# Mask halves half a batch earlier from the middle of the loop on, and another order of bias, ReLU and residual in the last tile

## The chip, the cores and the metric

The kernel runs on one core of a Trainium2 chip. Such a core has a matrix engine (TensorE, in the profile PE), three engines for elementwise work (VectorE or DVE, ScalarE or ACT, GpSimd or POOL), a queue that only issues transfers (SyncE or SP), and 16 DMA engines. All of them work through their own list of instructions in order, and wait for each other by semaphores. The metric is the device time of one execution in microseconds (us): the median of the runs.

## The reference

A layer of graph attention on x [16 batches, 512 nodes, 512 features], a conditioning vector per batch and an integer mask [16, 512, 512, 11]. Only the first 20 nodes of each batch are attended to.

```python
row_zero = exp_v.sum(-1) == 0
q_exp = jnp.where(row_zero[..., None], 0.0, q[:, None, :])
self_feat = concatenate([exp_v, q_exp], -1) @ W_self.T + b_self
output = self_feat
for d in range(2):
    A = adj_f if d == 0 else jnp.swapaxes(adj_f, 1, 2)
    A = A[:, :, :NONGT, :]                 # NONGT = 20
    cond = A.sum(-1)
    vb = A @ w_bias + b_bias
    output = output + _gat_attention(self_feat, cond, vb, ...)
return exp_v + jax.nn.relu(output)

# _gat_attention, 16 heads of 32, kv = self_feat[:, :20]
aff = jnp.einsum('bnhd,bmhd->bnhm', qh, kh) * (1.0 / np.sqrt(dh))
aff = jnp.where(cond_adj[:, :, None, :] > 0, aff, NEG) + label_bias[:, :, None, :]
w = jax.nn.softmax(aff, axis=-1)
out = jnp.einsum('bnhm,bmf->bnhf', w, kv) @ Wout + bout
```

So each batch needs the self features, the scores of 512 nodes against 2 x 16 x 20 keys, an additive mask from the integers, a softmax over each group of 20, the weighted sum of value rows, and at the end bias, ReLU and the addition of x.

## The kernel before

Features lie on the 128 partitions: a batch of x is a tile of 128 x 4 x 512 (four feature chunks, 512 nodes). A setup stage of about 107 us folds the weights into per-batch keys (`g`, kept in device memory as `g_d`) and per-batch value rows (`vw_d`). Then the main loop goes over 16 batches `b` and, in each, over four stages `nt` of 128 nodes. A mask half `(b, h)` covers two stages: half 0 the stages 0 and 1, half 1 the stages 2 and 3.

The order of the work is written out by hand: the calls of the loop body are recorded in program order, and each engine gets its own instructions in that order. What a stage issues is, in this order:

- SP: `store()` of finished output (L338), then loads. In stage 0 the rows of x for the row sums of batch b+2 (`load_xn`, L89). In stage 1 the mask half (b+1, 0) (`load_adj`, L93), then the per-key bias (`load_cq`, L100), and in batch 0 also `clear_blocks` (L126, six DMAs) and `blocks` (L142, twelve DMAs), which lay out all batches' value rows in `bd_d`. In stage 2 the values (`load_values`, L114), the keys of b+1 (L108), x of b+2 (L85) and the mask half (b+1, 1).
- `normal` of the stage before: VectorE sums the exponentials and takes reciprocals (L291, L292), POOL multiplies (L293).
- TensorE: `self_feat` (L186), the products for self features; in stages 0 and 1 for the second half of the nodes of this batch, in stage 3 for the first half of the nodes of the next. In stage 2 also `attend` (L311) of the batch before, into four banks, followed by `finish` (L324 on VectorE, L330 on ScalarE). Then `scores` (L246).
- mask work. `mask_mul`: ScalarE casts the integers (L207), POOL multiplies them by `w_bias` (L208). `mask_count`: VectorE counts (L213) and turns the count into 0 or a very negative number (L214). `mask_add`, a stage later: VectorE sums the products (L220) and adds the count's part (L222), ScalarE spreads the result over `both` (L227).
- `self_copy`: VectorE moves self features out of PSUM, adding the conditioning term (L199). The scores of later stages read them.
- `weigh` and `expo`: VectorE adds the mask, takes the maximum and subtracts it (L257, L259, L261), ScalarE exponentiates (L266).
- `turn` of the stage before: VectorE transposes the weights (L300); `full_add` for the next stage on POOL (L236), which joins `cq` and `both`; in stages 2 and 3 `residual` on POOL (L333), which adds x.

Buffers that matter: `ps_s` (scores) has two, `ps_acc` four. The four of `ps_acc` are shared by the results of `self_feat` and the four banks of `attend`. Mask integers (`adj`) have three, their products (`prod`) one, `both` two.

The last tile is the output of batch 15, after the loop. `attend` is split in two parts: nodes 0 to 383 from the first three stages and nodes 384 to 511 from the last. VectorE adds self features to each bank (L685), ScalarE adds the bias `bo` and applies ReLU (L689), then x is added: on POOL for chunks 0 to 2 of the first part (L692), on VectorE for the second part (L695) and for chunk 3 of the first (L698). All stores are issued by SP.

Of the kernel before, what the change touches and what calls it, by code (L numbers as in the profile page):

```python
# [9 lines left out]
AF = mybir.ActivationFunctionType  # L10
ALU = mybir.AluOpType
# [7 lines left out]
def gat_kernel(  # L19
# [20 lines left out]
    nc = tc.nc  # L40
    B, F, N = xT.shape
    NG, L = adj.shape[3], adj.shape[4]
    H, DH = 16, 32
    C = F // P
    HL = P // DH
    NT = N // P
# [10 lines left out]
    load = ctx.enter_context(tc.tile_pool(name="load", bufs=2))  # L57
# [7 lines left out]
    bo = const.tile([P, C], F32, name="bo")  # L65
# [13 lines left out]
    xs, xns, rss, adjs, nzs, sfs, cqs, gs, vds = {}, {}, {}, {}, {}, {}, {}, {}, {}  # L79
# [11 lines left out]
    def load_adj(b, h):  # L91
        t = adjs[b, h] = load.tile([P, 2, S * L], I32, tag="adj", name=f"adj{b}_{h}", bufs=3)
        nc.sync.dma_start(  # L93
            t, adj[b, h * 2 * P : (h + 1) * 2 * P].rearrange("(t p) d m l -> p t (d m l)", p=P)
        )
# [108 lines left out]
    def mask_mul(b, h):  # L204
        a = adjs[b, h]
        p = prods[b, h] = msk.tile([P, 2 * S, L], F32, tag="prod", name=f"prod{b}_{h}", bufs=1)
        nc.scalar.copy(p.rearrange("p m l -> p (m l)"), a.rearrange("p t m -> p (t m)"))  # L207
        nc.gpsimd.tensor_mul(p, p, wb_sb.unsqueeze(1).to_broadcast([P, 2 * S, L]))  # L208

    def mask_count(b, h):  # L210
        a = adjs.pop((b, h))
        cond = conds[b, h] = msk.tile([P, 2 * S], F32, tag="cond", name=f"cond{b}_{h}")
        nc.vector.tensor_reduce(cond, a.rearrange("p t (m l) -> p (t m) l", l=L), AX.X, ALU.add)  # L213
        nc.vector.tensor_scalar(cond, cond, 0.0, NEG, ALU.is_le, ALU.mult)  # L214

    def mask_add(b, h):

        nm = 2 * S
        lb = msk.tile([P, nm], F32, tag="lb", name=f"lb{b}_{h}")
        nc.vector.tensor_reduce(lb, prods.pop((b, h)), AX.X, ALU.add)  # L220
        add = msk.tile([P, nm], F32, tag="add", name=f"add{b}_{h}")
        nc.vector.scalar_tensor_tensor(add, conds.pop((b, h)), bb_sb, lb, ALU.add, ALU.add)  # L222

        both = adds[b, h] = msk.tile([P, 2, 2, S], F32, tag="both", name=f"both{b}_{h}")
        for a in range(2):
            for g in range(2):
                nc.scalar.copy(  # L227
                    both[bass.ts(a, R), :, g], add[bass.ts(g, R)].rearrange("p (t m) -> p t m", t=2)
                )
# [344 lines left out]
    with tc.manual_schedule():  # L574
        load_keys(1)

        prev = None
        o = None
        banks = None
        for b in range(B):  # L580
            def ahead(nt):


                if nt < 2:
                    return ((b, nt, 1),)
                return ((b + 1, 0, 0), (b + 1, 1, 0)) if nt == 3 and b + 1 < B else ()

            for nt in range(NT):
                store()
                if nt == 0 and b + 2 < B:  # L590
                    load_xn(b + 2, 0)
                    load_xn(b + 2, 1)
                if nt == 1:
                    if b + 1 < B:
                        load_adj(b + 1, 0)
                        load_cq(b + 1)
                    if b == 0:
                        clear_blocks(zero)
                        blocks()
                if nt == 2:  # L600
                    load_values(b)
                    if 0 < b < B - 1:
                        load_keys(b + 1)
                    if b + 2 < B:
                        load_x(b + 2)
                    if b + 1 < B:
                        load_adj(b + 1, 1)

                if prev is not None:
                    normal(*prev)  # L610
                ps = ps_s.tile([P, 2, 512], F32, tag="s", name=f"ps_s{b}_{nt}")
                for part in ahead(nt):
                    self_feat(*part)
                if nt == 2 and b > 0:
                    banks = [ps_acc.tile([P, 512], F32, tag="acc", name=f"ps_o{b - 1}_{q}") for q in range(4)]
                    for n in range(2):
                        attend(b - 1, n, [t[:, bass.ts(n, N // 2)] for t in banks])
                    o = work.tile([P, C, N], F32, tag="o", name=f"o{b - 1}")
                    finish(b - 1, o, (0, 1), banks)
                for g in range(2):  # L620
                    scores(b, nt, g, ps)

                if nt == 0:
                    mask_mul(b, 1)
                    mask_count(b, 1)
                if nt == 1:
                    mask_add(b, 1)
                if nt == 2 and b + 1 < B:
                    mask_mul(b + 1, 0)
                    mask_count(b + 1, 0)  # L630
                if nt == 3 and b + 1 < B:
                    mask_add(b + 1, 0)
                last = b == B - 1
                for part in ahead(nt):
                    self_copy(*part)
                if nt == 3 and b + 2 < B:
                    row_mask(b + 2)
                if last and nt == NT - 1:
                    s = soft.tile(full, F32, tag="s", name=f"s{b}_{nt}", bufs=3)
                    weigh_half(b, nt, ps, s, 0)  # L640
                    turn(*prev)
                    weigh_half(b, nt, ps, s, 1)
                else:
                    s = weigh(b, nt, ps)
                    expo(s)
                    if prev is not None:
                        turn(*prev)
                if nt < NT - 1:
                    full_add(b, nt + 1)
                elif b + 1 < B:  # L650
                    full_add(b + 1, 0)
                if nt >= 2 and b > 0:
                    residual(b - 1, 2 * nt - 4, o)
                    residual(b - 1, 2 * nt - 3, o)
                if b + 2 < B:
                    if 0 < nt < 3:
                        row_sum(b + 2, 2 * nt - 2)
                        row_sum(b + 2, 2 * nt - 1)
                    if nt == 3:
                        load_nz(b + 2)  # L660
                prev = (b, nt, s)
        store()
        b = B - 1
        turn_half(*prev, 0)
        turn_half(*prev, 1)

        o = work.tile([P, C, N], F32, tag="o", name=f"o{b}")
        out_b = out[b].rearrange("(c p) n -> p c n", p=P)
        most = [ps_acc.tile([P, 512], F32, tag="acc", name=f"ps_o{b}_{q}") for q in range(4)]
        pairs = [ps_s.tile([P, 2, 512], F32, tag="s", name=f"ps_o{b}_{q}_2") for q in range(2)]  # L670
        rest = [pairs[q // 2][:, q % 2] for q in range(4)]
        parts = []
        for lo, hi, banks in ((0, NT - 1, most), (NT - 1, NT, rest)):
            width = (hi - lo) * R
            parts.append((slice(2 * lo, 2 * hi), slice(lo * P, hi * P), width, banks))
            for n in range(2):
                attend(b, n, [t[:, bass.ts(n, width)] for t in banks], slice(lo, hi))
        for ts, ns, width, banks in parts:
            for q in range(4):
                c = bass.ds(q // 2 * 2, 2)  # L680

                def of(t):
                    return t[:, c].rearrange("p c (t q n) -> p c t q n", q=2, n=32)[:, :, ts, q % 2]

                nc.vector.tensor_add(  # L685
                    of(o), banks[q][:, : 2 * width].rearrange("p (c t n) -> p c t n", c=2, n=32), of(sfs[b])
                )
            for c in range(C):
                nc.scalar.activation(o[:, c, ns], o[:, c, ns], AF.Relu, bias=bo[:, c : c + 1])  # L689
        ns = parts[0][1]  # L690
        for c in range(3):
            nc.gpsimd.tensor_add(o[:, c, ns], o[:, c, ns], xs[b][:, c, ns])  # L692
            nc.sync.dma_start(out_b[:, c, ns], o[:, c, ns])
        ns = parts[1][1]
        nc.vector.tensor_add(o[:, :, ns], o[:, :, ns], xs[b][:, :, ns])  # L695
        nc.sync.dma_start(out_b[:, :, ns], o[:, :, ns])
        ns = parts[0][1]
        nc.vector.tensor_add(o[:, 3, ns], o[:, 3, ns], xs[b][:, 3, ns])  # L698
        nc.sync.dma_start(out_b[:, 3, ns], o[:, 3, ns])


# [44 lines left out]
```

## Time and profile before

| | |
|---|---|
| median of 3 runs | 647.06 us |
| lowest and highest run | 645.69 and 651.63 us |
| the profiled execution | 648.63 us |
| its span, first to last instruction | 646.5 us |
| busy: PE, DVE, POOL, ACT | 627.9, 522.8, 337.0, 217.4 us |
| mean granted clock of TensorE | 0.986 |
| one batch in the loop | 33.3 us |

Busy time is the time in which an engine executes an instruction; the weight loads of TensorE have their own row, PEld, and run beside its products. The page cuts the span into 40 slices of about 16 us and gives a digit for each: the busy share in tenths, or the granted clock in tenths of full speed. Lines of the timeline have the start, the length, the engine, the line of the kernel, the operation, what it writes and reads, and in brackets the idle time just before it and what ended it. Instructions of one kind in close succession are merged in such a line. The chain that ended last is followed back from the last instruction, at each step to what released it.

### The profile page before, as it was taken

How to read it: one execution, taken by the hardware profiler on the slowest of the kernel's cores; microseconds unless marked ns; L12 is line 12 of the kernel's file. 1: busy time of each engine (PE TensorE's matmuls, PEld its weight loads, DVE VectorE, ACT ScalarE, POOL GpSimd, SP SyncE). 2: the span in 40 equal slices, each digit the busy share in tenths (PEclk: the TensorE clock that was granted, in tenths of full speed). 3: DMA queues.
4: the chain of work that ended last, by engine and by line, in shares of the span. 5: the costliest groups of instructions: out<-in, count | busy, mean ns of one | idle time of the engine just before them, and what ended most of it. 6: DMA issues, size and time to landing. Idle time of an engine off the chain costs nothing.

```text
span 646.5 us, 16155 instructions
## 1 busy us (share of the span) xinstructions
PE 627.9 (97%) x6742; PEld 378.7 (59%) x6742; DVE 522.8 (81%) x802; ACT 217.4 (34%) x468; POOL 337.0 (52%) x254
## 2 busy tenths in 40 slices
PE   9998989999999999999999999999999999999992
PEld 7653336876656565656565656565656565656552
DVE  0644472899899898989898989898989898989896
ACT  0342341324233342425242425252525151523232
POOL 1420222442838374757474756556565647474754
PEclk9898998999999999999999999999999999999997
DMA  8939998766646464647464757475656566634112
GB/s 316 398 127 327 390 379 286 226 174 219 218 153 212 160 221 151 233 142 230 151 224 154 238 154 240 154 240 153 230 164 220 175 208 186 207 122 144 66 67 99
DMA packets 89888, 131.86 MB, mean 204 GB/s; under 512 B 9208, under 2 KB 59928, under 8 KB 87768
## 3 DMA queue, kind: packets, MB, share of 16 engines
q1 hardware_dynamic: 89144, 129.47, 60.0%
q0 software_dynamic: 672, 1.36, 0.8%
q8 instruction: 53, 0.87, 0.5%
q14 instruction: 19, 0.16, 0.1%
HBM read 90.89 MB, written 39.92 MB: 202 GB/s over the span
## 4 chain that ended last, share of the span: by engine, by line
PE 82%; DVE 2%; DMA 1%; ACT 1%; issue 0%; SPq 0%; DVEq 0%; ACTq 0%
PE ps_s L246 42%; PE ps_sf L186 32%; PE ps_o L311 6%; PE ps_g L518 1%; DMA g_d<-st 1%; ACT o L689 0%; DVE st L527 0%; SPq L532 0%; PE ps_v L492 0%; DVE s L284 0%; DVE mx L275 0%; DVE o L685 0%; DVE s L276 0%; DVE ps_s L273 0%; DVE wt L300 0%
## 5 line engine op out<-in xcount | busy, mean ns | idle before, releaser
L246 PE MATMUL ps_s<-g,sf 128*64 128x320 f32 x2048 | 289.1, 433 | 0.0
L186 PE MATMUL ps_sf<-x,ws_v 128*64 128x256 f32 (+1 forms) x2048 | 225.2, 372 | 0.0
L246 PEld LDWEIGHTS ps_s<-g,sf 128*64 128x64 f32 x2048 | 154.8, 137 | 118.0 <-issue 6.2
L186 PEld LDWEIGHTS ps_sf<-x,ws_v 128*64 128x64 f32 x2048 | 149.1, 137 | 71.9 <-issue 4.2
L293 POOL TENSOR_TENSOR s<-s,sm 128x640 f32<-128x640 f32 x63 | 80.2, 1273 | 151.0 <-DVE sm L292 133.5
L266 ACT ACTIVATE s<-s 128x640 f32<-128x640 f32 x63 | 46.5, 738 | 239.7 <-DVE s L261 239.7
L236 POOL TENSOR_TENSOR full<-cq,both 128x640 f32<-128x640 f32 x64 | 99.1, 1550 | 23.5 <-ACT both L227 23.5
L208 POOL TENSOR_TENSOR prod<-prod,wb_sb 128x880 f32<-128x880 f32 x32 | 61.4, 1918 | 60.9 <-ACT prod L207 60.9
L257 DVE TENSOR_TENSOR ps_s<-ps_s,full 128x640 f32<-128x640 f32 x63 | 52.3, 830 | 42.6 <-PE ps_s L246 42.5
L333 POOL TENSOR_TENSOR o<-o,x 128x512 f32<-128x512 f32 x60 | 75.3, 1277 | 0.0
L227 ACT COPY both<-add 64x80 f32<-64x80 f32 x128 | 32.8, 256 | 75.9 <-DVE add L222 74.8
L527 DVE TENSOR_SCALAR st<-ps_g 128x640 f32<-128x640 f32 x32 | 26.4, 824 | 37.8 <-PE ps_g L518 31.7
L291 DVE TENSOR_REDUCE sm<-s 128x32 f32<-128x640 f32 x63 | 51.7, 820 | 6.0 <-ACT s L266 0.9
L199 DVE SCALAR_TENSOR_TENSOR sf<-nz,qw,ps_sf 128x236 f32<-128x236 f32 (+1 forms) x128 | 52.6, 458 | 2.8 <-PE ps_sf L186 2.6
L259 DVE TENSOR_REDUCE mx<-ps_s 128x32 f32<-128x640 f32 x63 | 51.9, 825 | 2.2
L261 DVE TENSOR_TENSOR s<-ps_s,mx 128x640 f32<-128x640 f32 x63 | 51.9, 824 | 2.2
L300 DVE STREAM_TRANSPOSE wt<-s 128x640 f32<-128x640 f32 x63 | 52.5, 834 | 0.0
L311 PE MATMUL ps_o<-wt,vd 32*32 32x256 f32 (+2 forms) x2176 | 46.3, 374 | 5.6 <-issue 3.3
L330 ACT ACTIVATE o<-o,bo 128x512 f32<-128x512 f32 x60 | 40.0, 714 | 27.4 <-DVE o L324 24.9
L311 PEld LDWEIGHTS ps_o<-wt,vd 32*32 32x32 f32 x2176 | 31.0, 103 | 21.3 <-issue 13.8
L324 DVE TENSOR_TENSOR o<-ps_o,sf 128x512 f32<-128x512 f32 x60 | 36.3, 666 | 0.0
L525 ACT ACTIVATE st<-ps_g 128x640 f32<-128x640 f32 x32 | 22.4, 704 | 37.4 <-PE ps_g L518 29.5
(70 smaller groups left out, 422.1 us busy)
## 6 DMA issues: line engine op xcount, KB each, us to landing
g<-g_d SPq DMA_DIRECT2D x15, 1280.0 KB, 7.1
g_d<-st SPq DMA_DIRECT2D x16, 1120.0 KB, 6.1
x<-in_xT SPq DMA_DIRECT2D x16, 1024.0 KB, 9.2
out_T<-o SPq DMA_DIRECT2D x61, 256.0 KB, 2.0
xn<-in_xn SPq DMA_DIRECT2D x28, 512.0 KB, 6.7
adj<-in_adj SPq DMA_DIRECT2D x32, 440.0 KB, 8.1
vd<-bd_d SPq DMA_DIRECT2D x64, 128.0 KB, 2.6
nz<-nz_d SPq DMA_DIRECT2D x14, 256.0 KB, 4.5
```

Source lines behind the costliest of these rows:

```text
L186: nc.tensor.matmul(held[0][bass.ts(a, R), i * N // 2 : i * N // 2 + hi - lo], ws_v[:, k, bass.ds((2 * f + i) * P + a * R, R)], xs[b][:, k, ...
L199: nc.vector.scalar_tensor_tensor(sfs[b][:, 2 * f + i, lo:hi], nzs[b][:, lo:hi], qw[:, 2 * f + i, b : b + 1], ps[:, i * N // 2 : i * N // 2 ...
L208: nc.gpsimd.tensor_mul(p, p, wb_sb.unsqueeze(1).to_broadcast([P, 2 * S, L]))
L236: nc.gpsimd.tensor_add(f, cqs[b].unsqueeze(1).to_broadcast(shape), adds[b, nt // 2][:, nt % 2].unsqueeze(2).to_broadcast(shape),)
L246: nc.tensor.matmul(ps[bass.ts(a, R), g, : W // 2], sfs[b][:, k, bass.ds(nt * P + g * R, R)], keys[:, k, a], start=(k == 0), stop=(k == C - 1),
L257: nc.vector.tensor_add(pw, pw, fulls.pop((b, nt)).rearrange("p g h m -> p g (h m)"))
L259: nc.vector.tensor_reduce(mx, p4, AX.X, ALU.max)
L261: nc.vector.tensor_sub(s, p4, mx.unsqueeze(3).to_broadcast(full))
L293: nc.gpsimd.tensor_mul(s, s, sm.unsqueeze(3).to_broadcast(full))
L300: nc.vector.transpose(wts[b][:, nt], s.rearrange("p a h m -> p (a h m)"))
L311: nc.tensor.matmul(banks[q][bass.ts(e, DH)].rearrange("p (t n) -> p t n", n=32), vds[b][r, e, i, q // 2 * 2 + n], wt[r, :, bass.ts(j, 32)] ...
L333: nc.gpsimd.tensor_add(o[:, c], o[:, c], xs[b][:, c])
```

## The change

A table, `mask_plan`, is made ahead of the loop. It says for each stage which mask half is loaded, which is multiplied and counted, and which is added. Up to batch 7 it gives each half the stages it had. Batch B // 2 = 8 takes a third half, so that from there on every half comes half a batch earlier; in batch 15 there is none left. In a stage of batch 8 that has both, the addition comes ahead of the next half's multiplication and count. The loads of the table are made after the other loads of the stage: in stage 1 after `load_cq`, and in batch 0 after `clear_blocks` and `blocks`.

In the last tile ScalarE writes self features plus bias into `o` ahead of time, for all four chunks. VectorE then adds the banks to `o`. Chunks 0 to 2 of the first part have ReLU on ScalarE and x added on POOL as before; the second part and chunk 3 of the first have ReLU and the addition of x in one VectorE operation (`scalar_tensor_tensor`, maximum with 0, then add). The store of the second part is issued by ScalarE.

```diff
+        mask_plan = {(b, nt): [] for b in range(B) for nt in range(NT)}
+        m = 1
+        for b in range(B):
+            for nt in (0, 1, 2) if b == B // 2 else (0, 2):
+                if m < 2 * B:
+                    half = (m // 2, m % 2)
+                    if m > 1:
+                        mask_plan[(b, nt - 1) if nt else (b - 1, 2)].append(("load", half))
+                    mask_plan[b, nt].append(("mul", half))
+                    mask_plan[b, nt + 1].insert(0, ("add", half))
+                    m += 1
...
                 if nt == 1:
                     if b + 1 < B:
-                        load_adj(b + 1, 0)
                         load_cq(b + 1)
                     if b == 0:
                         clear_blocks(zero)
                         blocks()
...
-                    if b + 1 < B:
-                        load_adj(b + 1, 1)
+                for what, m in mask_plan[b, nt]:
+                    if what == "load":
+                        load_adj(*m)
...
-                if nt == 0:
-                    mask_mul(b, 1)
-                    mask_count(b, 1)
-                if nt == 1:
-                    mask_add(b, 1)
-                if nt == 2 and b + 1 < B:
-                    mask_mul(b + 1, 0)
-                    mask_count(b + 1, 0)
-                if nt == 3 and b + 1 < B:
-                    mask_add(b + 1, 0)
+                for what, m in mask_plan[b, nt]:
+                    if what == "add":
+                        mask_add(*m)
+                    elif what == "mul":
+                        mask_mul(*m)
+                        mask_count(*m)
...
         o = work.tile([P, C, N], F32, tag="o", name=f"o{b}")
+        for c in range(C):
+            nc.scalar.activation(o[:, c], sfs[b][:, c], AF.Identity, bias=bo[:, c : c + 1])
...
                 nc.vector.tensor_add(
-                    of(o), banks[q][:, : 2 * width].rearrange("p (c t n) -> p c t n", c=2, n=32), of(sfs[b])
+                    of(o), banks[q][:, : 2 * width].rearrange("p (c t n) -> p c t n", c=2, n=32), of(o)
                 )
-            for c in range(C):
-                nc.scalar.activation(o[:, c, ns], o[:, c, ns], AF.Relu, bias=bo[:, c : c + 1])
+
+        def end(queue, cs, ns):
+            nc.vector.scalar_tensor_tensor(
+                o[:, cs, ns], o[:, cs, ns], 0.0, xs[b][:, cs, ns], ALU.max, ALU.add
+            )
+            queue.dma_start(out_b[:, cs, ns], o[:, cs, ns])
+
         ns = parts[0][1]
         for c in range(3):
+            nc.scalar.activation(o[:, c, ns], o[:, c, ns], AF.Relu)
             nc.gpsimd.tensor_add(o[:, c, ns], o[:, c, ns], xs[b][:, c, ns])
             nc.sync.dma_start(out_b[:, c, ns], o[:, c, ns])
-        ns = parts[1][1]
-        nc.vector.tensor_add(o[:, :, ns], o[:, :, ns], xs[b][:, :, ns])
-        nc.sync.dma_start(out_b[:, :, ns], o[:, :, ns])
-        ns = parts[0][1]
-        nc.vector.tensor_add(o[:, 3, ns], o[:, 3, ns], xs[b][:, 3, ns])
-        nc.sync.dma_start(out_b[:, 3, ns], o[:, 3, ns])
+        end(nc.scalar, slice(0, C), parts[1][1])
+        end(nc.sync, slice(3, C), ns)
```

## The prediction

> **What bounds the kernel now.** I read the page's engine row first, then the clock row, then the chain that ended last.
>
> ```profile
> PE 627.9 (97%) x6742; PEld 378.7 (59%) x6742; DVE 522.8 (81%) x802; ACT 217.4 (34%) x468; POOL 337.0 (52%) x254
> PEclk9898998999999999999999999999999999999997
> PE 82%; DVE 2%; DMA 1%; ACT 1%; issue 0%; SPq 0%; DVEq 0%; ACTq 0%
> ```
>
> The chain is TensorE (PE) for 82% of the span, at full granted clock from the eighth slice to the last but one. So in the batch loop an instruction saved on another engine is worth nothing, and an instruction added costs only where TensorE then waits. Two places decide: stretches where VectorE (DVE) is nearly late, and the tail after the last scores (about 630 us), where the chain leaves TensorE. VectorE's spare time in the loop is 42.5 us of waiting for scores over 45 waits, just under 1 us a time.
>
> One batch takes 33.3 us, so batch 0 starts at about 107 us and batch 8 at about 373 us. Next I read the SP queue at the start of the loop, since the diff moves a load there (start, length, engine, line, operation, count).
>
> ```profile
> 111.45 0.44 SPq L93 DMA_DIRECT2D adj<-in_adj  x1
> ...
> 113.98 6.65 SPq L126 DMA_DIRECT2D bd_d<-zero  x6
> 120.80 9.42 SPq L142 DMA_DIRECT2D bd_d<-vw_d  x12
> 132.48 1.72 SPq L114 DMA_DIRECT2D vd<-bd_d  x4
> ...
> 134.72 0.50 SPq L93 DMA_DIRECT2D adj<-in_adj  x1
> ```
>
> The load of mask half (1,0) is issued at 111.45, ahead of the 18 DMAs of `clear_blocks` and `blocks`; these hold the queue until 130.22. Then VectorE over the same batches:
>
> ```profile
> 124.75 1.01 DVE L213 TENSOR_REDUCE cond<-adj 128x80 f32<-128x880 int32 x1
> ...
> 132.21 1.56 DVE L199 SCALAR_TENSOR_TENSOR sf<-nz,qw,ps_sf 128x236 f32<-128x236 f32 x4
> ...
> 140.98 1.07 DVE L213 TENSOR_REDUCE cond<-adj 128x80 f32<-128x880 int32 x1 [1.10 <-DMA adj<-in_adj]
> 142.08 1.92 DVE L214 TENSOR_SCALAR cond<-cond 128x80 f32<-128x80 f32 x1
> ...
> 150.70 0.86 DVE L199 SCALAR_TENSOR_TENSOR sf<-nz,qw,ps_sf 128x256 f32<-128x256 f32 x2
> ```
>
> At 124.75 VectorE reads half (1,0). Apart from the 1.10 us for half (1,1), it works without a pause until 151.56, when the self copy of (1,1,1) ends. TensorE:
>
> ```profile
> 138.00 0.43 PE L246 MATMUL ps_s<-g,sf 128*64 128x320 f32 x1
> ...
> 150.59 0.63 PE L311 MATMUL ps_o<-wt,vd 32*32 32x256 f32 x6
> 151.66 2.69 PE L311 MATMUL ps_o<-wt,vd 32*32 32x256 f32 x122 [0.44 <-issue]
> ```
>
> Scores of batch 1 start at 138.00; `attend(0)` starts at 150.59, stops after a few matmuls and goes on at 151.66, 0.1 us after that self copy. The reason is in the code: `attend` takes all four buffers of `ps_acc`, and the fourth still holds ps_sf(1,1,1). So here VectorE already sets TensorE's time, with no slack at all.
>
> **Part 1, the load of half (1,0).** In the new loop the loads of the plan stand behind the `nt == 1` block. For every batch that puts the mask load behind two cq loads, 2 us later, which costs nothing: in batch 7 it is issued at 341.80 and read at 358.71. In batch 0 it also puts it behind `clear_blocks` and `blocks`: 18 DMAs, 6.65 + 9.42 us of issue. When does it land? The queue loses the load's own 0.49 us and the 0.7 us for which a clear waited for that load to land, so it ends between 129.0 and 130.2; I take 129.2. From issue to landing no row shows this load alone. Below: 2.6 us (vd, 128 KB). Above: 6.3 us (issue 134.72, read 140.98, behind vd and 1 MB of x). Taking out that megabyte at the page's best rate of 398 GB/s, 2.6 us, and adding 0.4 us for the last bd_d packets gives 4.1 us. So it lands at 133.3, between 131.6 and 136.5.
>
> VectorE comes to its count at 124.75 and now waits until 133.3. Queued behind it are `weigh(0,2)`, `normal(0,2)`, the mask sum, the four self copies of batch 1 and all that follows; ScalarE waits at the cast of the same half, and POOL behind that cast. From the count to the self copy's end at 151.56 the old trace has 26.81 us, 1.10 of it the DMA wait, which goes since half (1,1) then lands first. The 1.92 us of the second L214 instead of 0.51 lies beside POOL's product of 1.91 us that the same landing released; it moves to half (1,0), so it stays in the sum. New end: 133.3 + 25.7 = 159.0. TensorE's own way there: it stops after self_feat at 138.0, since the first self copy now comes at 132.21 + 8.6 + 1.4 + 0.4 = 142.6; from there 4.3 + 3.5 + 4.3 us of work bring it to 154.7, where it waits again until 159.0. Against 151.56: **+7.5 us** (+5.7 to +10.6 by the landing). Behind that point TensorE runs without a pause in the old trace and VectorE falls in step with it, so nothing is won back.
>
> Here a rule counts. The page "TensorE: Matmul & The Clock Gate" of the Trainium skill (sections "Why this matters for your kernels" and "Part 1") says that after an idle gap of over about 3 us the array drops to half clock, and comes back after a window of about 3.4 us. The trace has gaps of up to 1 us in the loop and a full clock there, so it shows neither. By the row alone the two new gaps (4.6 and 4.3 us) cost what was summed. By the rule the first costs up to 1.7 us more, hidden in the second gap; a drop after the second gap would add 1.7 us. Since a drop in the first shortens the second to 2.6 us, I leave it out and keep it for the range.
>
> **Part 2, batch 8 takes three halves.** Per half VectorE has 1.01 + 0.5 (count) and 1.01 + 0.55 (sum), ScalarE 0.91 + 1.06, POOL 1.92.
>
> ```profile
> 383.43 0.86 DVE L199 SCALAR_TENSOR_TENSOR sf<-nz,qw,ps_sf 128x256 f32<-128x256 f32 x2
> ...
> 385.00 2.75 PE L311 MATMUL ps_o<-wt,vd 32*32 32x256 f32 x128
> ```
>
> In stage 1 the count of half (9,0) now stands ahead of this self copy, the one that `attend` waits for: it ends at 384.29 + 1.3 = 385.6 instead, 0.5 us after `attend` wants its fourth buffer. Half (9,0) is issued at 374.17 as before, and at the median landing of 8.1 us is there at 382.3, before the count at 383.4; at the longest, 9.9 us, it adds 0.7. In stage 2 some 2 us are added on VectorE, but the self copies of batch 9 end at 401.25 + 2 = 403.3 and the scores want them at 406.2. **+0.5 us** (0 to 1.5). From batch 9 each stage has the load it had, one half earlier; the copies of `both` wait for a `full_add` issued at the end of the stage before, which ends at 379.1 against copies at 383.6. Batch 15 has no mask work in stages 0 and 1, but there VectorE waited for scores anyway (0.9 us at each): nothing gained.
>
> **Part 3, the tail.**
>
> ```profile
> 637.50 2.82 DVE L685 TENSOR_TENSOR o<-ps_o,sf 128x384 f32<-128x384 f32 x8
> 638.52 3.30 ACT L689 ACTIVATE o<-o,bo 128x384 f32<-128x384 f32 x8 [3.92 <-DVE o L685]
> 639.21 2.90 POOL L692 TENSOR_TENSOR o<-o,x 128x384 f32<-128x384 f32 x3 [4.97 <-ACT o L689]
> ...
> 641.85 0.81 DVE L695 TENSOR_TENSOR o<-o,x 128x512 f32<-128x512 f32 x1 [1.53 <-ACT o L689]
> ...
> 643.16 0.53 SPq L699 DMA_DIRECT2D out_T<-o  x1
> ```
>
> The four new bias operations (0.65 to 0.71 each, as in L330) run on ScalarE from 634.6 to 637.3, idle until 638.52, before the adds of 637.50: free; without that cover they would cost up to 2.8. Five ScalarE ReLUs go, and VectorE's 1.53 us wait. The two fused operations, at the 0.81 and 0.54 us of the adds that they replace (0.85 by twice the 256-wide L199), end at 641.7. But the third POOL add still ends at 642.1, and its store and then the last one go out on SP in order: the last issue is at 642.5 instead of 643.16, **-0.6 us**. No row has a store from ScalarE's queue; below, it takes SP's 0.38 us of issue and is long gone; above, a slow first use of 1 us would still end with the rest. -1.0 to 0.
>
> Sum: 7.5 + 0.5 - 0.6 = +7.4. The profiled execution took 648.63 us (span 646.5), so 656.0 like it; it lies 1.6 us above the median, so the median becomes 647.06 + 7.4 = 654.5.
>
> **Rivals.** (a) Only the first gap counts: if the fourth buffer comes free sooner, TensorE loses 138.0 to 142.6 and no more: +4.6 - 0.1, 651.6. The stop at 151.66 speaks against it. (b) Clock: the second gap drops the clock, or the load lands late: 654.5 + 1.7 = 656.2 up to 660. (c) Not slower: the 18 DMAs pass the queue faster without the load ahead of them, and the load lands in time. TensorE is untouched as long as it lands by 124.75 + 1.1 = 125.9, so it must be issued by 121.8; then only 0.5 - 0.6 is left, 647.0. Against it: that asks 7.4 us off 16.1 us of issues, and the waits among them that the trace names sum to about 3.4 us, most on the same x and key loads as before. (d) The shift does what it is named for, a lighter last batch: the loop's slack says this gives nothing; at most VectorE's 0.4 us lag at 630.27 goes: within 1 us of (c).
>
> **How the numbers follow.** The forecast as summed has 0.60 (651.6 to 660), (a) 0.12, (b) 0.16, (c) with (d) 0.09, something else 0.03. The range 650.5 to 659.5 leaves out (c) and the far ends. A measurement of this kernel tells about 1% from no change, 6.5 us, so the line lies at 653.5, just under the forecast: two thirds of the forecast, nearly all of (b), little of (a) lie above it: slower 0.61, within 1% 0.36, faster 0.03.
>
> **What would show it.** In the profile after: a wait of VectorE L213 on the DMA of adj near 125 us of some 8.5 us; the issue of adj behind the last bd_d DMA near 129 us; gaps of TensorE near 138 and 155 us; `attend(0)` in full run near 159 us; batches at 33.3 us thereafter; last store issued 0.6 us earlier after the last matmul. The prediction is wrong if that wait is under 5 us, if TensorE's stop ahead of `attend(0)` is missing, or if batch 8 takes over 2 us more.

## The result and the profile after

The changed kernel takes 656.14 us (median of 4 runs, 655.14 to 658.91) against 646.38 us for the kernel before in the same comparison (645.69 to 651.63). The ratio is 1.014, with a 95% interval from 1.010 to 1.018. The forecast was 654.5 us, 7.4 us more than before. The profiled execution is the slowest of the four: it took 658.91 us with a span of 657.1 us, 10.6 us more than before. In the last comparison below (e10) one execution of the kernel before is left out, since it ran in a slower state of the chip (669.78 us).

The setup is the same in both kernels, yet the first scores of batch 0 start at 107.49 us in the trace before and at 108.75 us in the trace after. So 1.26 of the 10.6 us lie ahead of everything that was changed, and times of the loop are compared below from the first scores of batch 0 on. From there to the end of the span it is 539.01 us before (646.5 - 107.49) and 548.35 us after (657.1 - 108.75): **+9.34 us**.

The timeline of the SP queue after, at the same place:

```profile
112.71 1.12 SPq L100 DMA_DIRECT2D cq<-cq_d  x2
113.88 7.05 SPq L126 DMA_DIRECT2D bd_d<-zero  x6
121.09 9.31 SPq L142 DMA_DIRECT2D bd_d<-vw_d  x12
130.44 0.61 SPq L93 DMA_DIRECT2D adj<-in_adj  x1
```

The load of half (1,0) is issued at 130.44 instead of 111.45, right behind the 18 transfers. VectorE after, with its self copies (L199) and counts (L213):

```profile
135.35 1.07 DVE L213 TENSOR_REDUCE cond<-adj 128x80 f32<-128x880 int32 x1 [9.26 <-DMA adj<-in_adj]
136.45 1.93 DVE L214 TENSOR_SCALAR cond<-cond 128x80 f32<-128x80 f32 x1
...
144.28 1.56 DVE L199 SCALAR_TENSOR_TENSOR sf<-nz,qw,ps_sf 128x236 f32<-128x236 f32 x4
...
151.66 1.01 DVE L213 TENSOR_REDUCE cond<-adj 128x80 f32<-128x880 int32 x1
152.71 0.51 DVE L214 TENSOR_SCALAR cond<-cond 128x80 f32<-128x80 f32 x1
...
159.91 0.86 DVE L199 SCALAR_TENSOR_TENSOR sf<-nz,qw,ps_sf 128x256 f32<-128x256 f32 x2
```

VectorE waits 9.26 us for the load. The count of half (1,1) no longer waits, and the long L214 has gone over to half (1,0). TensorE after:

```profile
136.02 3.84 PE L186 MATMUL ps_sf<-x,ws_v 128*64 128x256 f32 x31
144.83 6.01 PE L246 MATMUL ps_s<-g,sf 128*64 128x320 f32 x32 [4.97 <-issue]
...
158.53 0.63 PE L311 MATMUL ps_o<-wt,vd 32*32 32x256 f32 x6
160.87 4.02 PE L311 MATMUL ps_o<-wt,vd 32*32 32x256 f32 x122 [1.71 <-issue]
```

There are two gaps, one ahead of the scores of batch 1 (4.97 us) and one within `attend(0)` (1.71 us). The second ends at 160.87, 0.1 us after the self copy on VectorE ends (159.91 + 0.86 = 160.77), just as 151.66 followed 151.56 before. The first scores behind the first gap take 6.01 us instead of about 4.5, and `attend(0)` behind the second 4.02 us instead of 2.69. The stretch from 140 to 174 us of the trace after shows why (columns: stretch, its length, busy time and instructions of PE, PEld, DVE, ACT, POOL, then granted clock, DMA share, GB/s):

```profile
140.00:174.00 34.00, 27.46 (x306) 16.52 (x308) 32.36 (x50) 13.80 (x33) 15.04 (x11) 0.90 0.46 136
```

The granted clock is 1.00 in the stretches of 33 us on both sides. A mean of 0.90 over 34 us is two windows of 3.4 us at half clock; the trace's clock record has them from 144.5 to 147.9 and from 161.5 to 164.9.

In batch 8 `attend(7)` takes 3.29 us instead of 2.75:

```profile
395.57 3.29 PE L311 MATMUL ps_o<-wt,vd 32*32 32x256 f32 x128
```

And in the tail the two fused VectorE operations take 2.59 us together, with POOL's three additions beside them:

```profile
650.26 3.35 POOL L710 TENSOR_TENSOR o<-o,x 128x384 f32<-128x384 f32 x3 [4.94 <-ACT o L709]
651.44 2.59 DVE L702 SCALAR_TENSOR_TENSOR o<-o,x 128x512 f32<-128x512 f32 x2
```

The account of the profile after, from the first scores of batch 0, has four terms:

- TensorE goes on in `attend(0)` after 52.12 us (160.87 - 108.75) instead of 44.17 (151.66 - 107.49): +7.95.
- Half clock in `attend(0)`: +1.33 (4.02 - 2.69).
- Batch 8: +0.54. The scores of stage 2 start 11.11 us later than before (398.79 against 387.68), the products of stage 1 10.57 us later (387.71 against 377.14).
- The tail, from the first bank addition to the end of the span: 8.51 us (657.1 - 648.59) instead of 9.0 (646.5 - 637.5), -0.49.

The sum is +9.33. From batch 8 to the tail nothing changes: the first bank addition comes 249.80 us after these scores of stage 2, before 249.82 us.

### The profile page after: what moved, and what is told of

The parts are those of the page before. It is cut to its first block, busy times and chain, and to the rows that moved or that the text cites. A ratio compares the mean times of both kernels' runs of the same rounds, so it can differ in the third digit from the quotient of the medians.

```text
span 657.1 us, 16155 instructions
## 1 busy us (share of the span) xinstructions
PE 632.2 (96%) x6742; PEld 378.6 (58%) x6742; DVE 523.5 (80%) x802; ACT 218.2 (33%) x467; POOL 337.4 (51%) x254
## 4 chain that ended last, share of the span: by engine, by line
PE 76%; DVE 3%; DMA 3%; SPq 2%; issue 1%; ACT 1%; DVEq 0%; ACTq 0%
PE ps_s L246 39%; PE ps_sf L186 29%; PE ps_o L311 6%; SPq L142 1%; DMA xn<-in_xn 1%; DMA g_d<-st 1%; PE ps_g L518 1%; DMA adj<-in_adj 1%; SPq L89 1%; DVE st L527 0%; DVE o L697 0%; DVE ps_s L257 0%; DVE s L261 0%; DVE mx L259 0%; ACT s L266 0%
## 5 line engine op out<-in xcount | busy, mean ns | idle before, releaser
L246 PEld LDWEIGHTS ps_s<-g,sf 128*64 128x64 f32 x2048 | 152.5, 138 | 126.6 <-issue 12.9
L311 PE MATMUL ps_o<-wt,vd 32*32 32x256 f32 (+2 forms) x2176 | 48.1, 384 | 6.9 <-issue 4.5
L199 DVE SCALAR_TENSOR_TENSOR sf<-nz,qw,ps_sf 128x236 f32<-128x236 f32 (+1 forms) x128 | 52.4, 457 | 2.8 <-PE ps_sf L186 2.6
L311 PEld LDWEIGHTS ps_o<-wt,vd 32*32 32x32 f32 x2176 | 32.0, 105 | 23.0 <-issue 14.6
L213 DVE TENSOR_REDUCE cond<-adj 128x80 f32<-128x880 int32 x32 | 33.1, 1038 | 9.3 <-DMA adj<-in_adj 9.3
```

Source lines behind the costliest of these rows:

```text
L199: nc.vector.scalar_tensor_tensor(sfs[b][:, 2 * f + i, lo:hi], nzs[b][:, lo:hi], qw[:, 2 * f + i, b : b + 1], ps[:, i * N // 2 : i * N // 2 ...
L246: nc.tensor.matmul(ps[bass.ts(a, R), g, : W // 2], sfs[b][:, k, bass.ds(nt * P + g * R, R)], keys[:, k, a], start=(k == 0), stop=(k == C - 1),
L311: nc.tensor.matmul(banks[q][bass.ts(e, DH)].rearrange("p (t n) -> p t n", n=32), vds[b][r, e, i, q // 2 * 2 + n], wt[r, :, bass.ts(j, 32)] ...
```

## The experiments

The theory was that all of the loss is one load behind 18 transfers, passed on by VectorE's late self copy. The rivals were that batch 8, the tail or later loads carry a share, and that there is a loss only beyond a threshold. In the diffs the `...` stand for unchanged lines.

**e1, the load back in its place.** The changed kernel with one edit.

```diff
                 if nt == 1:
+                    if b == 0:
+                        load_adj(1, 0)
                     if b + 1 < B:
                         load_cq(b + 1)
...
-                    if what == "load":
+                    if what == "load" and m != (1, 0):
```

> The changed kernel with one edit: in batch 0 the load of mask half (1,0) stands ahead of the cq load and of the 18 bd_d transfers again. Theory (all of the loss is this one load behind the 18 transfers): VectorE's 9.3 us wait for it near 126 us is gone, TensorE has no gap near 140 us, its clock stays full through the loop, and the time is that of the kernel before within 1 us: +0.5 us for batch 8, -0.5 us for the tail, together 646 to 647 us. Rival (the third mask half in batch 8 and the shorter lead of later loads carry part of the loss): 2 us or more above the kernel before.

Measured: 646.64 us against 648.55 us for the kernel before, ratio 0.998 (0.9962 to 0.9998). The trace of e1, VectorE:

```profile
124.30 1.01 DVE L213 TENSOR_REDUCE cond<-adj 128x80 f32<-128x880 int32 x1
...
140.65 1.07 DVE L213 TENSOR_REDUCE cond<-adj 128x80 f32<-128x880 int32 x1 [1.21 <-DMA adj<-in_adj]
```

The 9 us wait is gone. From the first scores of batch 0 (107.05) to the end of the span (646.3) it is 539.25 us, 0.24 us more than in the trace before: 0.1 in batch 0, 0.57 in batch 8 (scores of stage 2 at 387.91, 280.86 us after the first scores instead of 280.19, less that 0.1), and the tail at 8.56 instead of 9.0 us. So the mask plan and the tail, of which the one costs 0.57 and the other gains 0.44, together cost nothing that the medians show, and the whole loss hangs on this one line's place.

**e2, the load moved and nothing else.** The kernel before with one edit.

```diff
-                    if b + 1 < B:
-                        load_adj(b + 1, 0)
-                        load_cq(b + 1)
+                    if 0 < b < B - 1:
+                        load_adj(b + 1, 0)
+                    if b + 1 < B:
+                        load_cq(b + 1)
                     if b == 0:
                         clear_blocks(zero)
                         blocks()
+                        load_adj(1, 0)
```

> The kernel before with one edit: in batch 0 the load of mask half (1,0) is issued behind the 18 bd_d transfers. Mask plan and tail are the old ones. Theory: the whole loss comes back, 7.9 us of late VectorE work plus 1.3 us of half clock, so 9.3 us above the kernel before, 655 to 656.5 us, with a VectorE wait of 9 to 9.5 us near 126 us. Rival (other parts of the change carry a share): 5 to 7 us above.

Measured: 655.38 us against 648.55 us, ratio 1.0106 (1.0065 to 1.0146), so 6.8 us and not 9.3. VectorE, and TensorE's `attend(0)`, in the trace of e2:

```profile
131.34 1.07 DVE L213 TENSOR_REDUCE cond<-adj 128x80 f32<-128x880 int32 x1 [7.06 <-DMA adj<-in_adj]
```

```profile
140.82 6.22 PE L246 MATMUL ps_s<-g,sf 128*64 128x320 f32 x32 [2.77 <-issue]
...
156.86 2.70 PE L311 MATMUL ps_o<-wt,vd 32*32 32x256 f32 x122 [1.50 <-issue]
```

Here the load was issued at 127.78, 20.83 us after the first scores and not 21.69 as in the trace after, and read at 131.34, 3.56 us later and not 4.91. The second gap brought no half clock: `attend(0)` takes 2.70 us. The expectation took three chance terms of one execution (queue, landing, clock) for fixed ones. From the first scores (106.95) the loss to `attend(0)` is 5.74 us, and to the end of the span (651.7) 5.74 as well. Both figures lie where the rival put them, at 5 to 7 us; it falls all the same, by e1, in which the other parts cost 0.24 us, and by e5 below, in which the changed kernel itself loses 7.16 us. That the single line brings the loss is shown; how large it is differs from execution to execution.

**e3, the load behind 12 of the 18.** The kernel before, with the load taken out of its place as in e2 and put into `blocks`.

```diff
+        done = 0
...
                         nc.sync.dma_start(bb[:, r : r + hi - lo, e, i], vv[d, :, m : m + hi - lo, e])
+                        done += 1
+                        if done == 6:
+                            load_adj(1, 0)
```

> The kernel before with the load of half (1,0) issued after 6 of the 12 transfers of the second layout step, so behind 12 of the 18. Each of them takes 0.78 us of the queue, so the load is issued 4.7 us earlier than behind all of them and lands 4.9 us after issue. Theory (each us of landing beyond about 126 us after the span's start, counted as in the kernel before, is a us of TensorE time): VectorE waits 4 to 5 us, TensorE stops ahead of attend(0) for 3 to 4.5 us, 3.5 us above the kernel before without a clock drop, 4.8 us with one. Rival (a threshold: the loss appears only when TensorE's slack of 4 us at the scores of batch 1 is used up): within 1 us of the kernel before.

Measured: 653.51 us against 648.55 us, ratio 1.0069 (1.0041 to 1.0096). In this kernel the lines of VectorE and TensorE stand four further down (L217 is L213, L315 is L311).

```profile
129.81 1.07 DVE L217 TENSOR_REDUCE cond<-adj 128x80 f32<-128x880 int32 x1 [4.07 <-DMA adj<-in_adj]
```

```profile
139.29 4.53 PE L250 MATMUL ps_s<-g,sf 128*64 128x320 f32 x32
...
155.33 4.03 PE L315 MATMUL ps_o<-wt,vd 32*32 32x256 f32 x122 [2.90 <-issue]
```

There is no gap ahead of the scores of batch 1 now: VectorE's first self copy is there in time. The loss comes through the second place alone, 2.76 us to `attend(0)` and 1.34 of half clock behind it, 4.1 us in all. The rival that TensorE's slack at the scores covers the delay falls: at the fourth buffer of `ps_acc` there is none.

**e4, the second gap filled with work.** The changed kernel; 16 products are added whose results the scores overwrite.

```diff
+                if nt == 2 and b == 1:
+                    for _ in range(16):
+                        nc.tensor.matmul(
+                            ps[:R, 0, : W // 2], sfs[b][:, 0, :R], gs[b].rearrange(...)[:, 0, 0],
+                            start=True, stop=True,
+                        )
                 if nt == 2 and b > 0:
                     banks = ...
```

> The changed kernel with 16 additional TensorE products just ahead of attend(0), about 2.2 us of work at full clock whose results the scores overwrite. They fill the second TensorE stop (1.7 us near 159 us), which ends with VectorE's self copy whether they are there or not. Theory (the half clock from 161.5 to 164.9 us comes from the idle time of that second stop, and it lies on the path): granted clock 1.00 behind the stop, attend(0) in 2.7 us instead of 4.0, time 0.9 to 1.3 us under the changed kernel, 8.0 to 8.5 us above the kernel before. Rival (the second drop follows from the first, or from something other than idle time): the clock drops all the same and the time is that of the changed kernel or up to 0.5 us more.

Measured: 660.76 us against 648.55 us, ratio 1.0194 (1.015 to 1.0239): slower than the changed kernel, by neither theory. TensorE in the trace of e4:

```profile
138.97 4.53 PE L246 MATMUL ps_s<-g,sf 128*64 128x320 f32 x32 [3.33 <-issue]
...
151.06 8.78 PE L630 MATMUL ps_s<-g,sf 128*64 128x320 f32 x32
159.77 2.76 PE L311 MATMUL ps_o<-wt,vd 32*32 32x256 f32 x128
```

The filler takes 8.7 us, not 2.2. The trace has two rows for each product, and 2.2 us is what sixteen rows of the scores take (4.53 us for 32); that is one factor of two. For the other there is a reason in the code: the sixteen products of the scores alternate between the two halves of the array's columns and take 0.28 us each, the filler's all go to one half and take 0.54 us each. That the halves make the difference was not tested apart. VectorE's self copy ends at 154.9 and the filler at 159.8, so it outlasts the gap by about 5 us, and the run says nothing on the price of the drop. It does show a first gap of 3.33 us without any half clock behind it. Whether a filler of the right length keeps the clock up was not tried.

**e5, the changed kernel once more.** No edit.

> The changed kernel, unedited, once more. Law from the first experiments: the count of half (1,0) starts D later than in the kernel before (both counted from the first scores of batch 0), and TensorE goes on in attend(0) D - 1.39 us later; a half-clock window behind that adds 1.3 us. Theory: that law holds to 0.1 us here too, and D changes from run to run with the landing (3.6 to 4.9 us after issue so far), so D is 7 to 9.4 and the time 6.5 to 9.5 us above the kernel before. Rival (the changed kernel loses something that the single moved load did not show): attend(0) off that law by over 0.5 us, or over 1.5 us more lost after batch 0.

Measured: 652.66 us against 647.98 us, ratio 1.0078 (1.0051 to 1.0104). TensorE in its trace:

```profile
139.95 6.22 PE L246 MATMUL ps_s<-g,sf 128*64 128x320 f32 x32 [4.11 <-issue]
...
155.98 2.69 PE L311 MATMUL ps_o<-wt,vd 32*32 32x256 f32 x122 [1.49 <-issue]
```

One half-clock window, behind the first gap, none behind the second. D is 8.48 and TensorE goes on 7.08 us later, 1.40 us under D, on the expected law to 0.01 us. The rival, a further loss in the changed kernel, falls: the whole from the first scores (104.73) to the end of the span (650.9) is 7.16 us more than before. The median lies only 4.7 us above the kernel before, under the 6.5 to 9.5 that were expected; the setup, which is in the medians and not in these differences, varies by more than that from one execution to the next (last section).

The traces together, all from the first scores of batch 0 (us). D is how much later than before VectorE starts the count of half (1,0); L how much later TensorE goes on in `attend(0)`:

| kernel | D | L | D - L | half clock in `attend(0)` | to the end of the span |
|---|---|---|---|---|---|
| after | 9.34 | 7.95 | 1.39 | 1.33 | +9.34 |
| e5, after again | 8.48 | 7.08 | 1.40 | none | +7.16 |
| e2, load only | 7.13 | 5.74 | 1.39 | none | +5.74 |
| e3, behind 12 of 18 | 4.15 | 2.76 | 1.39 | 1.34 | +4.09 |
| e1, load back | -0.01 | 0.11 | | none | +0.24 |

For instance, after: the count starts 26.60 us after the first scores (135.35 - 108.75), before 17.26 (124.75 - 107.49). The loss follows the landing us by us, less 1.4 us, which is the wait for half (1,1), 1.10 us, and a little more that the kernel before lost there already in this one trace. In all seven traces in which `attend(0)` stops, TensorE goes on 0.10 or 0.11 us after the self copy of (1,1,1) ends.

The 1.4 us is itself a matter of landing. e6 and e8 below load the mask halves of batch 1 as the kernel before does. In e6 VectorE waited only 0.41 us for half (1,1), and `attend(0)` took 3.06 us in one piece (before, with its stop, 3.76); in e8 VectorE waited 2.10 us, and TensorE stopped for 1.42 us. The lines of e6:

```profile
143.70 1.07 DVE L213 TENSOR_REDUCE cond<-adj 128x80 f32<-128x880 int32 x1 [0.41 <-DMA adj<-in_adj]
...
154.01 3.06 PE L311 MATMUL ps_o<-wt,vd 32*32 32x256 f32 x128
```

So against another execution of the kernel before each loss in the table could be 0.7 us larger or 1.0 us smaller.

**e6, the last tile alone.** The kernel before with the tail part of the diff.

> The kernel before with the new last tile alone. Theory: from the first bank addition to the end of the span 8.5 us instead of 9.0; the two fused VectorE operations take 1.3 to 1.4 us each, not 0.81 and 0.54, so the last store is issued only 0.1 to 0.2 us earlier; the median is that of the kernel before within noise. Rival (in the tail a store on ScalarE's queue costs as a first use): span end later than 9.0 us after the first addition.

Measured: 647.15 us against 647.98 us, ratio 0.9996 (0.9975 to 1.0017). From the first bank addition (640.21) to the end of the span (648.7) 8.49 us; the last store is issued 5.50 us after that addition (645.71), before 5.66 us. The fused operations of e6:

```profile
L692 DVE SCALAR_TENSOR_TENSOR o<-o,x x2: 1343/1391/1439, 642.9 to 644.3; 128x512 f32<-128x512 f32 x1, 128x384 f32<-128x384 f32 x1
```

They take 1.3 to 1.4 us, as expected after the trace of the changed kernel. The rival, a dear first store from ScalarE's queue, falls. The loop of this execution was short by chance: from the first scores (110.91) to the end of the span it is 537.8 us, 1.2 less than in the trace before, of which the tail gives 0.5 and the missing stop in `attend(0)` 0.7.

**e8, the last tile without POOL.** e6 with one line less; chunks 0 to 2 of nodes 0 to 383 of batch 15 go out without x.

```diff
             nc.scalar.activation(o[:, c, ns], o[:, c, ns], AF.Relu)
-            nc.gpsimd.tensor_add(o[:, c, ns], o[:, c, ns], xs[b][:, c, ns])
             nc.sync.dma_start(out_b[:, c, ns], o[:, c, ns])
```

> The kernel before with the new last tile, without POOL's three additions of x (so chunks 0 to 2 of nodes 0 to 383 of the last batch go out without x). Theory A (the fused operations are slow because POOL reads the same memory beside them): they take 0.8 to 0.9 and 0.55 to 0.65 us. Theory B (the fused form itself costs more than an addition of the same size): they stay at 1.3 us each.

The trace of e8, the same line:

```profile
L692 DVE SCALAR_TENSOR_TENSOR o<-o,x x2: 550/622/693, 639.3 to 639.9; 128x512 f32<-128x512 f32 x1, 128x384 f32<-128x384 f32 x1
```

Without POOL's additions the fused operations take 0.69 and 0.55 us, so theory A holds as to what lengthens them: POOL's work beside them. That it is the reading of the same memory is argued only. The end of the span gains less than the operations: the last store is issued 4.20 us after the first bank addition (640.71 - 636.51) instead of the 5.50 of e6, and the span ends 8.1 us after it (644.6) instead of 8.5. The median, 647.28 us against 647.98 (ratio 0.9994, 0.9976 to 1.0011), does not tell.

**e9, both halves of batch 1 early.** What the traces point to: the kernel before lost about 1 us at the same place, by half (1,1). e6 with this edit:

```diff
                     if b + 1 < B:
                         load_adj(b + 1, 0)
+                        if b == 0:
+                            load_adj(1, 1)
                         load_cq(b + 1)
...
-                    if b + 1 < B:
+                    if 0 < b < B - 1:
                         load_adj(b + 1, 1)
```

> The kernel before with the new last tile, and with mask half (1,1) also loaded in stage 1 of batch 0, right behind half (1,0) and ahead of the cq load and the 18 bd_d transfers. Theory: the 1.10 us wait of VectorE for half (1,1) and the 1.9 us of L214 beside POOL's product are gone, VectorE is 2 us earlier at the self copy that attend(0) waits for, and TensorE's stop of 1 us there goes: 1.0 us less in the loop and 0.4 us less in the tail, 1.4 us under the kernel before. Rival (the second load delays the bd_d transfers, and with them the values that attend(0) reads): no gain, or up to 1 us loss.

Measured: 645.17 us against 647.98 us, ratio 0.9976 (0.995 to 1.0002), so not clear of 1. TensorE in the trace of e9:

```profile
142.15 4.64 PE L246 MATMUL ps_s<-g,sf 128*64 128x320 f32 x31
146.72 2.76 PE L311 MATMUL ps_o<-wt,vd 32*32 32x256 f32 x128
```

`attend(0)` runs through without a stop. From the first scores (103.62) to the end of the span (641.2) it is 537.58 us, 1.43 less than before, against 1.4 expected. But e6 without the early load took 537.8 us in its trace, so the 1.43 holds against that one trace of the kernel before. What is shown is that the stop is gone; how much that saves on average is not.

**e10, less for POOL in the last tile.** e9, in which VectorE also takes chunk 2.

```diff
-        for c in range(3):
+        for c in range(2):
...
-        end(nc.sync, slice(3, C), ns)
+        end(nc.sync, slice(2, C), ns)
```

> The kernel with both early loads and the new last tile, in which POOL adds x to chunks 0 and 1 only; chunk 2 of nodes 0 to 383 goes with chunk 3 into VectorE's second fused operation (768 elements wide). Theory (VectorE and POOL slow each other in the last 2.5 us, so less on POOL ends sooner): POOL ends 1.4 us earlier, the fused operations take 1.2 and 1.2 us, the last store is issued 5.1 us after the first bank addition instead of 5.5; from the first scores of batch 0 to the end of the span 537.2 us instead of 537.6, so 1.8 us less than in the kernel before. Rival (the total of additions is what counts, wherever it lies): last store at 5.5 us or later. Median 0.2 to 0.4% under the kernel before either way, which the rounds may just tell from none.

Measured: 646.24 us against 649.31 us (the median of 22 executions), ratio 0.9954 (0.9932 to 0.9976), clear of 1. The last store is issued 5.11 us after the first bank addition (640.10 - 634.99), as expected, but the span ends 8.71 us after it (643.7), later than in e9 (8.55); the last store is twice as large now. For the 2.0 us behind its issue (640.10 to 642.10) the 16 DMA engines are busy for 0.96 of the time, at 328 GB/s: what is left to do then is to move the output. That fits e8, where an issue 1.3 us earlier gained 0.4 to 0.5 us. From the first scores (105.99) the span is 537.7 us, as in e9, so the further step in the tail gave nothing.

Against the trace before that is 1.3 us, and the medians differ by 3.1. The rest is not explained by these traces. The setup, which is the same in both kernels, may have a part in it: the mean granted clock was 0.989 or more in 12 of the 18 executions of e10 and in 5 of the 22 of the kernel before.

## Why the prediction was right

**What bounds the kernel, and Part 1.** The step that carried the forecast held: TensorE sets the time, the one place with no slack is the fourth buffer of `ps_acc` at `attend(0)`, and the load behind 18 transfers reaches it through VectorE (e1, e2, e3). The queue was put at 21.7 us after the first scores (129.2 - 107.5) and took 21.7 (130.44 - 108.75). From issue to landing 4.1 us were estimated; five executions show 4.9, 4.1, 3.6, 4.4 and 3.8 us. The 25.7 us of VectorE work from the count to the self copy's end measure 25.4 us (135.35 to 160.77). The move of the long L214 to half (1,0) came as written. L was put at 7.5 and measured 7.95 and 7.08 in the two traces of this kernel.

**The clock.** This step failed. It took the gap of about 3 us that the Trainium skill gives ("TensorE: Matmul & The Clock Gate", "Why this matters for your kernels") as the bound, left out a drop behind the second gap, since a drop behind the first would shorten the second to 2.6 us, and kept 1.7 us for rival (b). In the trace after, the second gap was only 1.7 us and was followed by a half-clock window that cost 1.33 us on the path; in e5 a gap of 1.49 us at the same place was not. That the first drop is hidden in the second gap was right: the scores took 1.5 us more and the second gap was shorter for it. The sum of TensorE's own way also left out the first six products of `attend(0)`, 0.63 us, which run ahead of the stop and shorten it further; the end of the stop does not depend on them.

Against the trace after, the forecast was low by the landing (0.45) and by this term (1.33). Against the trace of e5 (+7.16) it was nearly exact. That its median lies between those of the two comparisons, which differ from the kernel before by 9.8 and 4.7 us, is in part luck: the clock term came in one of the two traces only, and the medians also have the scatter of the setup in them.

**Part 2, batch 8.** 0.5 us forecast; 0.54 in the trace after, 0.57 in e1, at the place named: the count of half (9,0) ahead of the self copy that `attend(7)` waits for. No gain in batch 15 was forecast and none was found (249.80 against 249.82 us above).

**Part 3, the tail.** -0.6 forecast, -0.45 to -0.5 measured, but not by the step given. It was to come from the last store's issue, since the fused operations were put at 0.81 and 0.54 us. The trace after shows 1.33 us each, and the last POOL addition 1.44 instead of 1.00, so the issue came only 0.16 us earlier (5.50 against 5.66 us after the first addition). The rest lies between the last issue and the span's end, 3.0 us instead of 3.3. In that stretch the output is moved: the DMA engines are busy nearly all the time from the last issue on, before 0.97 (643.16 to 645.00, at 322 GB/s), after as good as fully (654.09 to 655.70, at 355 GB/s). The store of the second part, 256 KB, is issued 4.25 us after the first addition (652.84 - 648.59) instead of 5.19 (642.69 - 637.50), so less is left to move at the end. That this gives the 0.3 us is argued, not tested. The four bias operations were free, as written.

**The rivals.** (a) falls by the stops at `attend(0)` in e2, e3 and e5. (b) is what the profiled execution did, in size 1.33 instead of 1.7, and what e5 did not do. (c) falls by VectorE's wait of 9.26 us, and by the queue's 9.31 us for the twelve transfers, as long as before (9.42). (d), a gain from a lighter last batch, did not show.

## What to carry to other kernels

A load that is moved in program order is moved past every transfer that its queue issues between the two places, in the one iteration too in which a block runs only once. To price it, follow the late operation to the buffer that is released last: here the obvious consumer, the scores of batch 1, had 4 us of slack (self copies done at 133.77, scores at 138.00 in the trace before), and the real one, a shared PSUM buffer, had none. And a loss that hangs on a queue and a landing is a range and not a number: one execution of the changed kernel lost 9.3 us and another 7.2, and the load alone cost 5.7.

## What the runs showed of the hardware

The half-clock windows of TensorE did not follow the length of the gap. Gaps of 1.71 us (after) and 2.90 us (e3) had one behind them, a gap of 3.33 us (e4) had none. Ahead of the end of the span all windows in the traces are 3.41 us long or twice that, and within one trace they start at whole multiples of 3.41 us from each other; in e4, for instance, at 58.51 and at 642.19, 171 x 3.413 us later. So one can lay this grid over each trace and ask how long TensorE idled in the stretch of 3.41 us just ahead of a possible window. In batch 1 a window followed 3.41, 2.93, 2.90, 2.33 and 1.71 us of idle time in such a stretch (first gap of after, e5, e3, first gap of e2, second gap of after), and none followed 1.95 (e4), 1.49 (e5), 1.42 (e8), 1.38 (e4) and 1.29 us (e2). What fits is that the part of a gap within one stretch of the grid counts, so that the same gap costs something or nothing by where it lies; this is read from the times and not tested. The idle time alone does not decide: 1.71 us had a window and 1.95 us had none. The products behind the two gaps differ (32 x 32 in the one, 128 x 64 in the other); whether that is the reason was not tested.

In the setup the number of these windows differs from execution to execution of kernels with the same setup, and the first scores of batch 0 start about 1.6 us later for each. With one window they start at 103.6 to 104.7 us (e9, e4, e5), with two at 105.5 and 106.0 (e8, e10), with three at 107.0 to 107.5 (e2, e1, before), with four at 108.4 and 108.8 (e3, after), with five at 110.9 (e6). That 7 us spread is nearly as wide as that of the whole times of the kernel before, 645.4 to 653.4 us in 51 executions. That the windows bring the later start is argued from this order alone, and what sets their number is open.

VectorE and POOL slowed each other when both added x in the tail: VectorE's fused operation of 512 elements took 1.1 to 1.4 us beside POOL in seven traces (1.08 in e5, 1.44 in e6) and 0.69 us without it (e8), and POOL's last addition of 384 elements 1.44 us instead of 1.00.
